# Adapter residual of the first pair: through memory as 32x32 squares instead of through TensorE

## Chip, cores and metric

One core of a Trainium2 chip runs the whole program. The metric is the device time of one execution in microseconds, the median of several runs. The engines work side by side, each through its own instructions in order: PE (TensorE, matrix products, with PEld for its weight loads), DVE (VectorE), ACT (ScalarE), POOL (GpSimd) and SP, which only issues transfers. Sixteen DMA engines move data between DRAM and the on-chip memory SBUF; matrix products land in the eight banks of PSUM.

## The reference

Four sequences of 512 tokens with 512 features pass through two layers. The first, in short:

```python
q, k, v = x @ Wq, x @ Wk, x @ Wv
attn_out = softmax(q @ k.T * scale) @ v @ Wp + bp
cms_out = gelu(attn_out @ cW1 + cb1) @ cW2 + cb2 + one_hot(target_codes)
modifier = gelu(concat([attn_out, cms_out]) @ mW1 + mb1) @ mW2 + mb2
out = clip(x + cms_out + modifier, 0, 1)
```

The second is an adapter with weights chosen per sequence (`stream`), and it is what the change touches:

```python
h = gelu(hidden_states @ Wd + bd)          # 512 -> 256
h = h @ Wu + bu                            # 256 -> 512
h = hidden_states + h                      # the residual
h = (h - mean) / sqrt(var + 1e-5) * g + b  # over the 512 features of a token
```

All data are float32.

## The kernel before

The four sequences are worked on in two pairs. After attention, each pair goes through four large layers (c1, c2, m1, m2 for cW1, cW2, mW1, mW2). Their products are made by a Strassen-like scheme: seven outer products p, in the order of `FIRST_C = (2, 1, 5, 6, 7, 3, 4)` for c1 and of `SECOND = (3, 1, 5, 6, 7, 2, 4)` for c2, each made of seven inner products q. A float32 product of 256 columns shows as two TensorE instructions in the profile. The activations are kept turned, features on the 128 partitions and tokens along the free dimension.

In the second pair's c1 layer each outer product is made by `c1_two_level` through `seven` (line 591). Per inner product TensorE writes two PSUM banks (rows r = 0, 1), in the order q = 1, 5, 6, 2, 7, 3, 4. Between them stands work of VectorE: `add(c15[r], ps, c1[r])` after q5, `add(y[r], x[r], c15[r])` after q6, which TensorE must await before q7 accumulates onto x, `add(v, x[r], c15[r])` after q7, which it must await before q4, and the adds of `keep` into the hidden blocks. In products 6 and 7 POOL adds as well (L1178), and it makes the weight sums of later products (L1140) and the token sums (L1087 to L1090). The first copies c1[r] are ACT's, except in products 3 and 4, where they are VectorE's (L612).

The adapters of the first pair run inside that layer. `adapters()` (L1718) gives a generator; `c1_layer` takes one step of it after q6, q7 and q4 of each product but the first, so steps 1 to 3 lie in product 1, 4 to 6 in product 5, 7 to 9 in product 6, 10 to 12 in product 7, 13 to 15 in product 3 and 16 to 18 in product 4. `adapter` (L1573) needs seven steps per sequence, and sequence 1 comes before sequence 0:

- two steps `down` (L1509): eight TensorE instructions of 512 columns each, then a gelu on ACT into g, which is `first`;
- one step `with_bias` (L1504): ACT adds b_up to the turned input, into the tile of the sequence in `cms`;
- four steps, one for each 128 tokens t: `up_product` (L1521) lets TensorE turn the 128x512 block of the residual into a PSUM bank by four products with the identity (L1526) and accumulates the up product onto it (L1531); `normalised` (L1558) reads the bank twice on VectorE, for the statistics (L1561, L1563) and for (h - mean) * g into `part` (L1564). `root` (L1544) takes one square root per tile on ACT, VectorE its reciprocal (L1566). For t < 3 `shifted` (L1552) scales on ACT (L1554), adds b on POOL (L1555), and POOL issues the output (L1556); for t = 3 VectorE does both (L1568) and POOL only issues (L1569).

ACT has to load a table whenever it changes between gelu and square root. The adapter weights of sequence 1 are in slot 4 and 5, those of sequence 0 in slot 6 and 7; the halves of slot 5 and 7 behind the first 1024 columns are free. The operand sums of the first c2 product are POOL's and go to slots 6 and 7 after product 3 (`second_operands`, L1331, by L206). The tile framework sets all semaphores and orders each engine's instructions by its own plan; `keep_in_program_order` pins an instruction in the order in which the code gives it. The transfers that the change adds go to POOL's and ACT's queues; those of the weights are SP's.

The second pair's own adapters, at the end of the program, use `adapter` and `last_adapter` and are not touched. `bias_rows` (L157) is a small tile for the biases of the first layer, turned once at the start by L168.

Of the kernel before, what the change touches and what calls it, by code (L numbers as in the profile page):

```python
# [1 line left out]

# [6 lines left out]
F32 = mybir.dt.float32  # L9
I32 = mybir.dt.int32  # L10
AF = mybir.ActivationFunctionType
ALU = mybir.AluOpType
# [6 lines left out]
def kernel(  # L19
# [38 lines left out]
    nc = tc.nc  # L58
# [3 lines left out]
    E, _, BN = W_down.shape  # L62
    P = 128
    NT = T // P
    NV = V // P
    NH = HID // P
    NB = BN // P
# [8 lines left out]
    const = ctx.enter_context(tc.tile_pool(name="const", bufs=1))  # L76
    small = ctx.enter_context(tc.tile_pool(name="small", bufs=4))
    spill = ctx.enter_context(tc.tile_pool(name="spill", bufs=1, space=DRAM))
    psum = ctx.enter_context(tc.tile_pool(name="psum", bufs=8, space=PSUM))

    def bank(name):
        return psum.tile([P, 512], F32, tag="bank", name=name)
# [7 lines left out]
    cms = [const.tile([P, 4, 512], F32, name=f"cms{i}") for i in range(2)]  # L90

    mod = [const.tile([P, 4, 512], F32, name=f"mod{i}") for i in range(2)]

    wide = const.tile([P, 8, 512], F32, name="wide")
    slot = [wide[:, 4 * i : 4 * i + 4, :].rearrange("p c n -> p (c n)") for i in range(2)]
    slot += [const.tile([P, 2048], F32, name=f"slot{i}") for i in range(2, 8)]
    wslot = [const.tile([P, 2048], F32, name=f"wslot{i}") for i in range(4)]
    part = const.tile([P, 4, 512], F32, name="part")
    first = const.tile([P, 2, 512], F32, name="first")
# [54 lines left out]
    bias_src = (bp, cb1, cb2, mb1, mb2)  # L154
    counts = [v.shape[0] // P for v in bias_src]
    nbias = sum(counts)
    bias_rows = const.tile([nbias, P], F32, name="bias_rows")  # L157
    at = 0
    for v, n in zip(bias_src, counts):
        nc.gpsimd.dma_start(  # L160
            out=bias_rows[at : at + n, :], in_=v.rearrange("(c p) -> c p", p=P)
        )
        at += n
    bias = const.tile([P, nbias], F32, name="bias")
# [18 lines left out]
    eps = const.tile([P, 1], F32, name="eps")  # L183
# [362 lines left out]
    def add(dst, a, b):  # L546
        nc.vector.tensor_tensor(dst, a, b, ALU.add)  # L547
# [220 lines left out]
        return left_operand(w, s)  # L768

    xT_kept = [spill.tile([P, 4, 512], F32, name=f"xT_kept{b}") for b in range(B)]  # L770
    attn_kept = [spill.tile([P, 4, 512], F32, name=f"attn_kept{b}") for b in range(B)]

    def softmax(k, lhs, rhs, then):
# [125 lines left out]
    ends = []  # L899
# [604 lines left out]
    def with_bias(y, bu, y1):  # L1504

        for c in range(NV):
            nc.scalar.activation(y1[:, c, :], y[:, c, :], AF.Identity, bias=bu[:, c : c + 1])

    def down(y, wd, bd, g, n, tokens=slice(0, 512)):  # L1509
        ps = bank("down_ps")[:, : tokens.stop - tokens.start]  # L1510
        for c in range(NV):
            nc.tensor.matmul(  # L1512
                ps,
                lhsT=wd[:, c, n * P : (n + 1) * P],
                rhs=y[:, c, tokens],
                start=(c == 0),
                stop=(c == NV - 1),
            )
        nc.scalar.activation(g[:, n, tokens], ps, AF.Gelu, bias=bd[:, n : n + 1])
# [53 lines left out]
    def adapter(b, y, loaded, g, rows, y1, eng):  # L1573
# [7 lines left out]
        for t in range(NT):  # L1581
            normalised(b, rows[:, t, :], up_product(g, wu, y1, t), aff, t, eng)
            yield

    def last_adapter(b, y, loaded, g, rows, y1, eng):


        wd, wu, bd, bu, aff = loaded
# [23 lines left out]
        for t in range(NT):  # L1612
            stats = small.tile([P, 2, 6], F32, name="stats")
            mv = small.tile([P, 2], F32, name="mv")
            pieces = []
            for i, columns in enumerate(both if t == NT - 1 else whole):
                ps = up_product(g, wu, y1, t, columns)
# [9 lines left out]
            rstd = scaled(t, pieces, mv)  # L1627
            if t == 0:
                shifted(b, rows[:, t, :], rstd, aff, t, eng)
            elif t == 1:  # L1630
                h = rows[:, t, :]
# [15 lines left out]
    def next_hidden():  # L1647

        h11, h12, h21, h22 = turned
        turned[:] = [h22, h11, h21, h12]  # L1650
        return list(turned)
# [5 lines left out]
    for pair in range(B // 2):  # L1657
        final = pair == B // 2 - 1

        h = next_hidden()  # L1660
# [21 lines left out]
        h = next_hidden()  # L1682
# [27 lines left out]
        loads = {}  # L1710
# [4 lines left out]
        def adapt(s, space, eng, pair=pair, loads=loads, kind=adapter):  # L1715
            return kind(2 * pair + s, cms[s], loads[s], *space, eng)

        def adapters(adapt=adapt):  # L1718
            for s in (1, 0):
                yield from adapt(s, (first, part, cms[s]), nc.gpsimd)  # L1720

        next_rhs = []

# [78 lines left out]
```

## Time and profile before

| | |
|---|---|
| median of three runs | 1170.36 us (1168.99 to 1171.34) |
| the profiled execution | 1169.93 us, of which its span 1168.2 us |
| instructions in it | 13,723 |
| mean granted TensorE clock | 0.999 |
| adapters of the first pair, from the first down to the last output issued | 693.8 to 784.9 us |
| end of the second pair's c1 layer on TensorE | 792.2 us |
| 128x128 turns by TensorE in this stretch (L1526) | 32 instructions |
| up products in it (L1531) | 32 instructions |
| ACT table loads at L1547 and L1039 in the whole program | 6 and 4, 1.28 us each |

Busy time is the time in which an engine has an instruction under way; TensorE's instructions overlap, so its busy time does not say that it runs at its peak, and the distance from the start of one group of instructions to the next is a better price. Idle time carries the name of what ended it. The timeline gives start and duration of instructions, neighbours of one line merged (x4 = four of them); the windows give the busy time of each engine in a stretch, with the number of instructions.

### The profile page before, as it was taken

Reading aid. Unit: us, or ns where it says so; the run is one execution under the profiler, and the core shown is the slowest. Engines: PE = TensorE matmul, PEld = TensorE weight load, DVE = VectorE, ACT = ScalarE, POOL = GpSimd, SP = SyncE. Lnnn points to the kernel's source line nnn. Section 1 sums busy time; section 2 is a strip of 40 time slices with the busy share of each in tenths; the row PEclk is TensorE's granted clock in tenths of the full one; section 3 lists DMA queues with packets and bytes.
Section 4 is the critical chain, followed back from the end, with each engine's and each line's share of the span. In section 5 each row is a group of like instructions: output and inputs, shape, how many; then the busy total and the mean of one; then the engine's idle time right before and its main releaser. Section 6 shows DMA issues by size and latency. Waiting matters only on the chain.

```text
span 1168.2 us, 13723 instructions
## 1 busy us (share of the span) xinstructions
PE 1158.7 (99%) x4989; PEld 927.4 (79%) x4989; DVE 893.8 (77%) x1215; ACT 293.2 (25%) x535; POOL 588.6 (50%) x652
## 2 busy tenths in 40 slices
PE   9999999999999999999999999999999999999997
PEld 8588558657468888888888887778888888888875
DVE  5755655587699967899699956689994588689956
ACT  4244315236520000012310027271000003220014
POOL 4989999988897058982200636972000001242101
PEclk9999999999999999999999999999999999999999
DMA  9742784897766588896847662135745454594701
GB/s 336 268 139 100 297 323 176 307 382 253 300 240 245 185 282 313 322 328 263 258 157 279 191 215 90 64 143 179 299 132 188 168 216 180 176 307 165 246 6 73
DMA packets 81283, 256.80 MB, mean 220 GB/s; under 512 B 7956, under 2 KB 38976, under 8 KB 65984
## 3 DMA queue, kind: packets, MB, share of 16 engines
q1 hardware_dynamic: 56864, 152.98, 36.4%
q0 software_dynamic: 21968, 93.37, 22.7%
q10 hardware_dynamic: 2384, 9.57, 2.1%
q8 instruction: 40, 0.66, 0.2%
q14 instruction: 27, 0.22, 0.1%
HBM read 186.69 MB, written 66.06 MB: 216 GB/s over the span
## 4 chain that ended last, share of the span: by engine, by line
PE 94%; DVE 2%; POOL 1%; DMA 1%; issue 1%; DVEq 0%
PE i L1406 29%; PE i L1306 26%; PE sum L1148 9%; PE sum L703 9%; PE sum L637 8%; PE c L1238 6%; PE down_ps L1512 2%; PE up_ps L1531 2%; PE tr_ps L489 1%; DMA wslot<-in_L_cond_mW 1%; PE up_ps L1526 1%; DVE slot L206 1%; DVE hidden L547 1%; PE tr_ps L868 0%; PE idle_ps L193 0%
## 5 line engine op out<-in xcount | busy, mean ns | idle before, releaser
L1306 PE MATMUL i<-slot,wslot 128*128 128x256 f32 x1184 | 261.4, 379 | 1.3 <-DVE part L1010 1.2
L1306 PEld LDWEIGHTS i<-slot,wslot 128*128 128x128 f32 x1184 | 224.7, 190 | 32.8 <-issue 1.8
L1406 PE MATMUL i<-slot,wslot 128*128 128x256 f32 x896 | 202.5, 379 | 0.0
L1406 PEld LDWEIGHTS i<-slot,wslot 128*128 128x128 f32 x896 | 170.2, 190 | 23.1
L1017 ACT COPY first<-i 128x256 f32<-128x256 f32 (+1 forms) x56 | 26.7, 477 | 516.0 <-PE i L1406 255.6
L1406 PE MATMUL i<-hidden,wslot 128*128 128x256 f32 x576 | 132.2, 379 | 0.0
L1406 PEld LDWEIGHTS i<-hidden,wslot 128*128 128x128 f32 x576 | 109.4, 190 | 15.7 <-issue 1.0
L1010 DVE TENSOR_TENSOR part<-i,part 128x512 f32<-128x512 f32 (+1 forms) x156 | 90.5, 591 | 37.7 <-PE i L1306 25.4
L1039 ACT ACTIVATE hidden<-hidden,bias 128x512 f32<-128x512 f32 x128 | 83.9, 716 | 81.3 <-DVE hidden L547 71.3
L1688 POOL DMA_DIRECT2D slot<-xT_kept x4 | 2.7, 683 | 152.9 <-PE i L1306 152.9
L1148 PE MATMUL sum<-mod,wslot 128*128 128x256 f32 x288 | 66.7, 379 | 0.2 <-DVE sum L547 0.2
L206 DVE TENSOR_TENSOR slot<-hidden 128x1024 f32<-128x1024 f32 x46 | 61.3, 1332 | 0.0
L1148 PEld LDWEIGHTS sum<-mod,wslot 128*128 128x128 f32 x288 | 54.6, 190 | 7.9 <-DVE sum L547 0.6
L1691 POOL TENSOR_TENSOR cms<-cms,slot 128x512 f32<-128x512 f32 x16 | 24.4, 1548 | 71.3 <-PE i L1306 41.1
L1010 DVE TENSOR_TENSOR part<-i,first 128x512 f32<-128x512 f32 (+1 forms) x62 | 36.3, 589 | 29.0 <-PE i L1306 17.7
L547 DVE TENSOR_TENSOR sum<-sum,wslot 128x512 f32<-128x512 f32 x48 | 33.3, 696 | 31.5 <-PE sum L703 19.6
L206 DVE TENSOR_TENSOR slot<-hidden,slot 128x1024 f32<-128x1024 f32 x46 | 56.8, 1234 | 0.3
L1238 PE MATMUL c<-slot,wslot 128*128 128x512 f32 x128 | 55.3, 592 | 0.0
L547 DVE TENSOR_TENSOR hidden<-part,hidden 128x2048 f32<-128x2048 f32 x20 | 54.6, 2732 | 0.5
L703 PE MATMUL sum<-hidden,wslot 128*128 128x256 f32 x232 | 53.4, 380 | 0.6 <-POOL wslot L201 0.6
L703 PEld LDWEIGHTS sum<-hidden,wslot 128*128 128x128 f32 x232 | 43.7, 190 | 6.7 <-POOL wslot L201 1.0
L1238 PEld LDWEIGHTS c<-slot,wslot 128*128 128x128 f32 x128 | 24.3, 190 | 30.6 <-issue 27.5
(338 smaller groups left out, 2129.3 us busy)
## 6 DMA issues: line engine op xcount, KB each, us to landing
wslot<-m_kept SPq DMA_DIRECT2D x48, 1024.0 KB
wslot<-m_kept SPq DMA_DIRECT2D x36, 512.0 KB
wslot<-c_kept SPq DMA_DIRECT2D x16, 1024.0 KB
slot<-in_L_cond_mW POOLq DMA_DIRECT2D x24, 512.0 KB
wslot<-in_L_cond_mW SPq DMA_DIRECT2D x24, 512.0 KB
wslot<-in_L_cond_cW SPq DMA_DIRECT2D x40, 256.0 KB
slot<-in_L_cond_cW POOLq DMA_DIRECT2D x16, 512.0 KB
m_kept<-wide POOLq DMA_DIRECT2D x6, 1024.0 KB
```

Source lines behind the costliest of these rows:

```text
L206: i = eng.tensor_tensor(out_, one, two, ALU.subtract)
L547: nc.vector.tensor_tensor(dst, a, b, ALU.add)
L637: nc.tensor.matmul(ps, lhsT=lhs[p][:, c, r * P : (r + 1) * P], rhs=rhs[p][:, c, :], start=(first_ and c == 0), stop=(c == 1), skip_group_c ...
L703: nc.tensor.matmul(v[:, j, :], lhsT=lhs[p][:, c, j * P : (j + 1) * P], rhs=rhs[p][:, c, :], start=(first_ and j == 0 and c == 0), stop=(c ...
L1010: nc.vector.tensor_tensor(dst, ps, other, ALU.add)
L1017: nc.scalar.copy(c1, p1)
L1039: nc.scalar.activation(block[:, t, :], block[:, t, :], AF.Gelu, bias=bias_c[:, 8 * half + t : 8 * half + t + 1],)
L1148: nc.tensor.matmul(halves_of(ps)[:, j, :], lhsT=a[g][:, at_[q], j * P : (j + 1) * P], rhs=rhs[q][:, 0, :], start=(first_ and j == 0), stop ...
L1238: nc.tensor.matmul(ps, lhsT=lhs(c, t), rhs=operands[p][:, c, :], start=(c == 0), stop=(c == 1),)
L1306: nc.tensor.matmul(out_ps[:, j, :], lhsT=a[j][q][:, c, :], rhs=now[q][:, c, :], start=(c == 0), stop=(c == 1),)
L1406: nc.tensor.matmul(ps[:, :256], lhsT=a[k // 2][q][:, k % 2, :], rhs=now[q][:, k, :], start=(k == 0), stop=(k == 3),)
L1691: nc.gpsimd.tensor_tensor(cms[s][:, d, :], cms[s][:, d, :], in_rows[3][:, d, :], ALU.add)
```

## The change

For the first pair the residual is no longer turned by TensorE. ACT adds b_up in place, POOL writes the turned sequence to a DRAM tile (`turn_kept`), and four loads issued from ACT, one for each 32 partitions, read it back such that each 32x32 square lies in the place that it has in the token-major block, but still mirrored. VectorE then turns the squares of a 128x512 block with one instruction and adds the up product from PSUM; statistics and scaling read SBUF afterwards. The sequences go in the order 0, 1, with both downs first. Mean and variance of the four tiles are gathered in one tile, and one square root and one reciprocal per sequence serve all four; the rest (`shifted`, for all four tiles now) follows while the next sequence's tiles are made, and in steps 15 to 17 for the last. g has a place of its own for each sequence, in the free halves of slots 5 and 7. The rows of sequence 1 go to the tile that held sequence 0. `bias_rows` becomes a part of `mod[1]`.

```diff
-    bias_rows = const.tile([nbias, P], F32, name="bias_rows")
+    bias_rows = mod[1][:nbias, 0, :P]
...
+    turn_kept = [
+        spill.tile([P, 4, 512], F32, name=f"turn_kept{k}").rearrange("p q n -> (p q) n")
+        for k in range(2)
+    ]
...
+    def load_squares(src, dst):
+        squares = src.rearrange("(i r) (d a c) -> a r d i c", r=32, a=4, c=32)
+        for a in range(4):
+            yield tc.keep_in_program_order(nc.scalar.dma_start(
+                out=dst[32 * a : 32 * a + 32].rearrange("p d (i c) -> p d i c", c=32),
+                in_=squares[a],
+            ))
+
+    def turned_adapters(two, space):
+        def first_half(b, y, loaded, g):
+            wd, wu, bd, bu, aff = loaded
+            for n in range(NB):
+                down(y, wd, bd, g, n)
+                if n == NB - 1:
+                    with_bias(y, bu, y)
+                    nc.gpsimd.dma_start(
+                        out=turn_kept[b % 2].rearrange("(c p) n -> p c n", p=P), in_=y
+                    )
+                yield
+
+        def reciprocal(rstd):
+            tc.keep_in_program_order(nc.vector.reciprocal(rstd, rstd))
+
+        def added(loaded, g, y, rows, t, mv):
+            wu, aff = loaded[1], loaded[4]
+            h = rows[:, t, :]
+            nc.vector.transpose(h, y[:, t, :])
+            ps = bank("up_ps")
+            for n in range(NB):
+                nc.tensor.matmul(
+                    ps, lhsT=g[:, n, t * P : (t + 1) * P], rhs=wu[:, n, :],
+                    start=(n == 0), stop=(n == NB - 1),
+                )
+            add(h, ps, h)
+            stats = small.tile([P, 6], F32, name="stats")
+            nc.vector.bn_stats(stats, h)
+            nc.vector.bn_aggr(mv[:, t, :], stats)
+            nc.vector.scalar_tensor_tensor(
+                h, h, mv[:, t, 0:1], aff[:, 0, :], ALU.subtract, ALU.mult
+            )
+
+        y1, y2 = two[0][1], two[1][1]
+        squares = chain(*(load_squares(turn_kept[b % 2], y) for b, y, _, _ in two))
+        yield from first_half(*two[0])
+        yield
+        for _ in first_half(*two[1]):
+            next(squares)
+            next(squares)
+            yield
+        yield
+        def end(n=1):
+            for _ in range(min(n, len(ends))):
+                ends.pop(0)()
+
+        ends = []
+        for i, rows in enumerate((space, y1)):
+            b, y, loaded, g = two[i]
+            mv = small.tile([P, NT, 2], F32, name="mvs")
+            for t in range(NT):
+                added(loaded, g, y, rows, t, mv)
+                if i == 0 and t < 2:
+                    next(squares)
+                    next(squares)
+                elif t == 2:
+                    end()
+                elif t == 3:
+                    end(4)
+                yield
+            rstd = small.tile([P, NT], F32, name="rstds")
+            nc.scalar.activation(rstd, mv[:, :, 1], AF.Sqrt, bias=eps)
+            ends = [partial(reciprocal, rstd)] + [
+                partial(shifted, b, rows[:, t, :], rstd[:, t : t + 1], loaded[4], t, nc.gpsimd)
+                for t in range(NT)
+            ]
+        yield
+        end()
+        yield
+        end(4)
...
-        def adapters(adapt=adapt):
-            for s in (1, 0):
-                yield from adapt(s, (first, part, cms[s]), nc.gpsimd)
+        def adapters(pair=pair, loads=loads):
+            g = [t[:, 1024:].rearrange("p (n k) -> p n k", n=NB) for t in (slot[5], slot[7])]
+            return turned_adapters(
+                [(2 * pair + s, cms[s], loads[s], g[s]) for s in (0, 1)], part
+            )
```

More of the change, by code (lines that the diff above doesn't have):

```diff
@@ L1 @@
 from contextlib import ExitStack
+from functools import partial
+from itertools import chain
 import concourse.bass as bass
```

## The prediction

> **What bounds the kernel now.** I read the page first, then the chain of waits, then the stretch in which the first pair's adapters run. Page, parts 1 and 4:
>
> ```profile
> PE 1158.7 (99%) x4989; PEld 927.4 (79%) x4989; DVE 893.8 (77%) x1215; ACT 293.2 (25%) x535; POOL 588.6 (50%) x652
> ...
> PE 94%; DVE 2%; POOL 1%; DMA 1%; issue 1%; DVEq 0%
> ```
>
> TensorE issues from end to end, so any TensorE instruction removed is worth its issue time, unless another engine takes the place. TensorE's timeline at one adapter tile gives that price (start, duration, line, operation; x4 = four instructions):
>
> ```profile
> 712.73 0.60 PE L1526 MATMUL up_ps<-ident,cms 128*128 128x128 f32 x4
> 713.17 1.88 PE L1531 MATMUL up_ps<-slot,first 128*128 128x512 f32 x4
> 714.89 1.89 PE L1148 MATMUL sum<-slot,wslot 128*128 128x256 f32 x8
> ```
>
> By starts, the four turns of a tile cost 713.17 - 712.73 = 0.44 us, the four up matmuls 714.89 - 713.17 = 1.72 us, and eight of the first layer's instructions 1.73 us. The windows of the last four products of the second pair's first layer (p = 6, 7, 3, 4) and of the layer behind show who stands next to TensorE (columns: PE, PEld, DVE, ACT, POOL busy, clock, DMA share, GB/s):
>
> ```profile
> 726.11:747.22 21.11, 21.11 (x82) 14.83 (x81) 15.34 (x25) 6.36 (x10) 20.29 (x23) 1.00 0.30 111
> 747.22:763.61 16.39, 16.39 (x73) 12.94 (x72) 9.94 (x16) 6.47 (x10) 16.16 (x19) 1.00 0.16 48
> 763.61:780.13 16.52, 16.52 (x73) 12.86 (x72) 14.51 (x29) 12.11 (x18) 14.22 (x18) 1.00 0.17 62
> 780.13:792.22 12.09, 12.09 (x57) 10.64 (x56) 11.97 (x22) 7.66 (x12) 7.86 (x5) 1.00 0.90 295
> 792.22:804.31 12.09, 12.09 (x58) 10.64 (x57) 12.09 (x11) 4.66 (x8) 2.98 (x2) 1.00 0.55 167
> ```
>
> VectorE has idle time in the first three (5.8, 6.4, 2.0 us) and none in p = 4 or behind it; POOL is 96 to 99% busy in the first two; the DMA engines are nearly empty until p = 4.
>
> **The change, part by part.** The sum is made against the profiled execution: span 1168.2 us, 1169.93 us as a run, 0.4 us under the median of 1170.36; differences are added to the median.
>
> *Turns removed.* 8 tiles x 0.44 = 3.5 us off TensorE. Nothing else of TensorE changes: 4 down products and 8 x 1.72 us of up matmuls stay, in another order: products 1 and 5 now hold all four downs (3.43 us each), products 6, 7, 3 hold 3, 3 and 2 tiles. Products 6 to 4 then take 4 x 12.08 + 8 x 1.72 = 62.1 us instead of 66.1.
>
> *VectorE per tile.* Today a tile costs these rows:
>
> ```profile
> 715.63 0.68 DVE L1561 BATCH_NORM_STATS2 stats<-up_ps 128x6 f32<-128x512 f32 x1
> 716.35 0.18 DVE L1563 BATCH_NORM_AGGREGATE mv<-stats 128x2 f32<-128x6 f32 x1
> 716.57 0.75 DVE L1564 SCALAR_TENSOR_TENSOR part<-up_ps,mv,slot 128x512 f32<-128x512 f32 x1
> ```
>
> That is 0.72 + 0.22 + 0.67 (start to start where back to back), plus a reciprocal of 0.15, and one shift of 0.74 to 1.64 per sequence (L1568). New are a transpose and an add from PSUM. The add is L547's: pairs take 1.28, so 0.61. No VectorE transpose is in this trace: the lower bound is 0.34 (half of the 0.68 of the 128x1024 TENSOR_SCALAR at L1467), the upper two passes, 1.22; I take 0.61, the one-source COPY of the same shape (L612, 0.66 to 0.68, 0.60 start to start). A new tile is 0.61 + 0.61 + 1.59 = 2.8 us.
>
> The Trainium skill ("VectorE: DVE Perf Modes", The three transpose paths, and its rules for authors) lists 311 ns for a 128x128 bf16 VectorE transpose and advises TensorE for 128x128 where PSUM may be the target, which speaks against this change. Four of its figures would be an estimated 1.24 us, and the sum below would be 5 us higher; no run so far shows which holds.
>
> *The scaling operation changes its source.* L1564 reads one SBUF tensor and PSUM today; now it reads two SBUF tensors. Two rows of the same operation with two SBUF tensors differ by what POOL does beside them:
>
> ```profile
> 736.43 1.64 DVE L1568 SCALAR_TENSOR_TENSOR part<-part,rstd,slot 128x512 f32<-128x512 f32 x1
> 783.32 0.74 DVE L1568 SCALAR_TENSOR_TENSOR part<-part,rstd,slot 128x512 f32<-128x512 f32 x1
> ```
>
> At 736.43 POOL was adding (L1178), at 783.32 it was idle. So each of the scalings can cost 0 to 0.9 us more; I take half, 0.45, for the six tiles of products 6 and 7, where POOL hardly rests: 2.7 us.
>
> *VectorE's account.* The first layer's own work in products 6 to 4 is 64 adds x 0.605 + 4 copies x 0.62 = 41.2 us. With 8 x 2.81 and two reciprocals it becomes 64.0, with contention 66.7. It can begin 2.6 us into product 6 (the first c15 add follows three half products of 0.86) and may end 2.1 us after TensorE, as today (792.22 against 794.36): 62.1 - 2.6 + 2.1 = 61.6 us. So it is 5.1 us over (2.4 without contention). Today the tiles of one sequence fell into product 5, which has idle time; the new order puts downs there and all eight tiles behind it. A further 1.5 us: VectorE waits for the up matmuls of a tile it is due to add, as it does now (three waits for up_ps, 3.4 us, between 726 and 795; about half taken).
>
> *Slack behind.* The second layer starts with a long block of pinned VectorE work, and its eight PSUM banks come back late (VectorE, then TensorE):
>
> ```profile
> 802.16 4.48 DVE L1326 TENSOR_TENSOR hidden<-hidden,hidden 128x2048 f32<-128x2048 f32 x2
> 806.56 0.41 DVE L1010 TENSOR_TENSOR cms<-i,cms 128x256 f32<-128x256 f32 x1
> 806.90 0.41 DVE L1010 TENSOR_TENSOR cms<-i,first 128x256 f32<-128x256 f32 x1
> ...
> 806.03 5.34 PE L1406 MATMUL i<-slot,wslot 128*128 128x256 f32 x24
> ```
>
> TensorE needs another bank at 806.03 + 2 x 1.73 = 809.5; the first one that this burst returns is free at 807.3. VectorE can be 2.2 us later than today before TensorE stops.
>
> *The detour through memory.* POOL issues two 1 MB writes, 0.56 us each as at L1556. ACT issues eight loads, 0.51 us each (the four of Wk took 2.06). Each load has 32 x 4 x 16 = 2048 runs of 128 bytes, 128 per DMA engine. The rows around that size: 80 packets of 4 bytes took 1.2% of 16 engines in 350 to 355 us, 12 ns each; 558 of 1 KB took 51.5% in 3 to 6 us, 44 ns each. So one load is 1.5 to 5.7 us of all engines; nearest is the small end, 16 ns, 2.1 us. The first sequence's last two loads stand behind its partner's bias on ACT: product 5 starts at 707.55, the second down ends at 707.55 + 8.63 + 2 x 3.43 = 723.0, gelu 0.69 and four times 0.72 end at 726.6, issue 1.0, then 2.2 us until data is usable (the first Wq quarter: issued 0.73, read 4.45, less 1.5 us for its and Wk's 0.5 MB at the 350 GB/s of that window), then 4.2 us: 734.0. The first tile is due when product 6 has run three of its seven parts, 726.5 + 5.2 = 731.7. Late by 2.3 us, which I take; bounds 1.2 (3.1 us of data) to 9.4 (11.3). What waits behind the first transpose on VectorE are product 6's remaining adds, and TensorE waits for these before q7. ACT, waiting for the second write, holds nothing until product 7's copies.
>
> The Trainium skill ("DMA: Bandwidth & Descriptors", Specifications) puts full line rate at 512 bytes and more, with read-modify-write below; the 4-byte row shows no such penalty in its record. By the page I would take the far end, 9.4 us late, and the sum would be 7.1 us higher.
>
> *At nothing:* six square roots and some four table loads less (1.28 us each, ACT is 39 to 73% busy in these products; no gain on the path either, though VectorE's two waits for rstd, 3.6 us, end); two more POOL adds and the moved output DMAs (POOL waits 5.3 us before L1569 today; without that cover the operand sums, 784.9 to 795.2, run later and could cost 2 us); the first down now needs cms0, complete at 681.5, for 693.8; bias_rows in mod1 (its transpose is done at 23.2, mod is first written at 26.1).
>
> **Sum.** -3.5 + (5.1 + 1.5 + 2.3 - 2.2) = +3.2 us: 1170.4 + 3.2 = **1173.6 us**.
>
> **The rivals.** *TensorE keeps its gain* (24%): the transposes move into VectorE's idle time, contention stays out, loads are in time. Then 2.4 us over is covered by the 2.2 us and the time is 1170.4 - 3.5 = 1166.9. For it: no wait of TensorE in this stretch today, and the deferred roots take VectorE's 3.6 us of waits away; against it: the account without any mishap already uses the slack up. *The gain is given back at the second layer* (12%): VectorE reaches 794.4 as today and paces what follows; 1170.4. For it: the 100% busy window behind 792. *The squares are slow* (14%): 1 KB-like packets or a write that waits behind POOL's sums (710.6 to 720) make the first tile 9.4 us late instead of 2.3: 1173.6 + 7.1 = 1180.7. It decides from a load time of 4 us each. Against it: empty DMA engines. That the turns don't vanish from TensorE has no ground: up_product isn't called on this path.
>
> **How the numbers follow.** The forecast, VectorE as bound of products 6 to 4, has 50%, from 1170.5 to 1178 (more contention, 8 x 0.9, gives +4.5; a transpose of 1.22 gives +3.7 on six tiles). About 0.2%, 2.3 us, is what a measurement tells from no change. Of the 50%, 13 lie below 1172.7; with the 12% that is 25% for the same; faster 24%; slower 37 + 14 = 51%. The range takes in the full gain with 1.1 us below it (the runs before lie 1.4 us under their median) and the slow loads up to their price: 1165.8 to 1180.8.
>
> **What would show it.** Right: L1526's first-pair instructions gone; VectorE above 95% busy from about 732 to 790; TensorE waiting for L547 or for a PSUM bank there; scalings with a spread from 0.74 to 1.6. Squares: ACT's loads land after VectorE's first transpose is due, and that wait is named DMA. Wrong: VectorE idle for more than 3 us in products 6 and 7, or TensorE without gaps up to 850 us and the whole 3.5 us won.

## The result and the profile after

The changed kernel takes 1173.48 us (median of 16 runs, 1171.06 to 1176.03), the kernel before 1168.95 us in its own 16 (1167.68 to 1171.34). The ratio is 1.0037, 95% interval 1.0028 to 1.0045: about 4.3 us slower. The profiled execution has a span of 1172.7 us against 1168.2. Lines move by a few: L547 is L549 now, L1148 is L1154, L1406 is L1412, L206 is L208, L1326 is L1332; the new lines are L1620 (transpose), L1623 (up product), L1629 and L1630 (statistics), L1631 (scaling), L1560 and L1561 (root's factor on ACT, b on POOL).

The turns are gone: TensorE runs 4957 instructions where it ran 4989, and product 6 begins at 726.56 us, 0.45 us later than before, as the two downs more and three tiles less ahead of it require (2 x 3.43 - 3 x 2.16 = 0.4). Then the windows of the stretch: product 6, product 7 up to the end of the wait and somewhat beyond, and the rest of 7 with half of 3 (columns: PE, PEld, DVE, ACT, POOL busy, clock, DMA share, GB/s):

```profile
726.00:743.20 17.20, 17.20 (x69) 12.92 (x68) 12.07 (x21) 4.03 (x8) 14.49 (x17) 1.00 0.71 153
743.20:760.50 17.30, 12.78 (x46) 9.61 (x45) 17.09 (x28) 5.07 (x7) 14.69 (x17) 0.86 0.32 90
760.50:776.00 15.50, 15.50 (x56) 11.20 (x56) 13.63 (x25) 4.46 (x7) 13.61 (x15) 0.93 0.16 51
```

Of these three, VectorE is full in the second alone. TensorE loses 4.5 us there, and its granted clock is under 1.00 in that window and the next, which it was nowhere in this stretch before. TensorE's timeline shows one wait (in brackets: idle before, and what ended it):

```profile
750.69 1.89 PE L1154 MATMUL sum<-slot,wslot 128*128 128x256 f32 x8
757.10 3.78 PE L1154 MATMUL sum<-mod,wslot 128*128 128x256 f32 x8 [4.52 <-DVE sum L549]
760.67 2.42 PE L1154 MATMUL sum<-slot,wslot 128*128 128x256 f32 x6
```

The same eight instructions take 1.89 us before the wait and 3.78 after it. VectorE's timeline shows what it did while TensorE waited:

```profile
747.03 1.29 DVE L1620 STREAM_TRANSPOSE part<-cms 128x512 f32<-128x512 f32 x2
...
749.87 1.81 DVE L1631 SCALAR_TENSOR_TENSOR part<-part,mvs,slot 128x512 f32<-128x512 f32 x1
...
753.26 0.78 DVE L1631 SCALAR_TENSOR_TENSOR part<-part,mvs,slot 128x512 f32<-128x512 f32 x1
753.97 1.29 DVE L1620 STREAM_TRANSPOSE cms<-cms 128x512 f32<-128x512 f32 x2
755.19 1.24 DVE L549 TENSOR_TENSOR mod<-sum,mod 128x512 f32<-128x512 f32 x2
756.36 1.28 DVE L549 TENSOR_TENSOR sum<-sum,mod 128x512 f32<-128x512 f32 x2
```

The last two rows are product 7's c15 and y additions, the ones TensorE needs for q7. In the code they stand ahead of the fourth tile and of the second sequence's transposes; the framework's plan has put both in front. So the 4.5 us are a matter of order as well as of load. The windows behind the wait, TensorE alone (busy, instructions, clock, DMA share, GB/s):

```profile
756.00:758.00 2.00, 0.90 (x2) 0.50 0.00 0
...
762.00:764.00 2.00, 2.00 (x7) 0.85 0.00 0
```

The fourteen instructions behind the wait take 762.93 - 757.10 = 5.8 us where 14 x 0.216 = 3.0 were due: 2.8 us that no part of the prediction had. From the first down to the start of c2 (the second pair's second layer) TensorE needs 102.30 us, before it was 98.44. The account: -3.5 for the turns, 4.5 to 4.7 for the wait (idle time, and from start to start), 2.8 for the clock, sum +3.8 to +4.0, measured +3.86. The rest, +0.65, lies in c2 and behind. There the new order leaves the second sequence's four b additions to POOL at the start of c2, beside VectorE's first operands:

```profile
798.27 3.92 DVE L1332 TENSOR_TENSOR wide<-hidden,hidden 128x2048 f32<-128x2048 f32 x1
802.11 2.28 DVE L208 TENSOR_TENSOR slot<-hidden 128x1024 f32<-128x1024 f32 x1
...
807.88 1.23 DVE L208 TENSOR_TENSOR slot<-hidden 128x1024 f32<-128x1024 f32 x1 [1.28 <-POOL cms L1561]
```

Before, the first took 3.00 and L206 1.21 each time, with no wait. VectorE's block behind them starts 14.0 us into c2 instead of 9.9.

The squares were in time. The first sequence's last load landed at 731.81 us, VectorE's first transpose ran at 732.55 with no wait for a DMA, and the DMA view of 700 to 760 us has:

```profile
q10 hardware_dynamic: 16512, 2.10, 22.3%
...
cms<-turn_kept ACTq DMA_DIRECT2D x8, 256.0 KB, 4.3
```

0.223 x 60 us x 16 engines / 16512 packets is 13 ns for a packet of 128 bytes, and the median load lands 4.3 us after its issue. The slowest took 9.5 us (740.09 to 749.57) and was still 4.4 us ahead of its transposes.

### The profile page after: what moved, and what is told of

Read it like the earlier page. It is cut to its first block, busy times and chain, and to the rows that moved or that the text cites. A ratio compares the mean times of both kernels' runs of the same rounds, so it can differ in the third digit from the quotient of the medians.

```text
span 1172.7 us, 13683 instructions
## 1 busy us (share of the span) xinstructions
PE 1158.0 (99%) x4957; PEld 925.6 (79%) x4957; DVE 898.7 (77%) x1223; ACT 288.3 (25%) x527; POOL 598.4 (51%) x656
## 4 chain that ended last, share of the span: by engine, by line
PE 84%; POOL 8%; DMA 3%; DVE 3%; issue 2%; SPq 0%; DVEq 0%; POOLq 0%
PE i L1312 28%; PE i L1412 27%; PE sum L639 7%; PE sum L1154 6%; PE c L1244 6%; PE sum L705 5%; PE down_ps L1518 2%; DMA wslot<-in_L_cond_mW 1%; PE up_ps L1537 1%; DMA c_outer<-part 1%; PE tr_ps L491 1%; POOL slot L208 1%; DMA wide<-in_L_cond_Wq 1%; POOL wide L200 1%; POOL wslot L1146 0%
## 5 line engine op out<-in xcount | busy, mean ns | idle before, releaser
L1412 PE MATMUL i<-slot,wslot 128*128 128x256 f32 x896 | 202.5, 379 | 0.0
L1412 PEld LDWEIGHTS i<-slot,wslot 128*128 128x128 f32 x896 | 170.2, 190 | 23.1
L1412 PE MATMUL i<-hidden,wslot 128*128 128x256 f32 x576 | 132.3, 379 | 0.1
L1412 PEld LDWEIGHTS i<-hidden,wslot 128*128 128x128 f32 x576 | 109.4, 190 | 16.2 <-issue 1.0
L1154 PE MATMUL sum<-mod,wslot 128*128 128x256 f32 x288 | 68.5, 387 | 4.5 <-DVE sum L549 4.5
L1154 PEld LDWEIGHTS sum<-mod,wslot 128*128 128x128 f32 x288 | 55.7, 194 | 13.1 <-DVE sum L549 4.9
L208 DVE TENSOR_TENSOR slot<-hidden 128x1024 f32<-128x1024 f32 x46 | 63.5, 1380 | 1.3 <-POOL cms L1561 1.3
L549 DVE TENSOR_TENSOR sum<-sum,wslot 128x512 f32<-128x512 f32 x48 | 33.3, 696 | 33.1 <-PE sum L705 21.2
L208 DVE TENSOR_TENSOR slot<-hidden,slot 128x1024 f32<-128x1024 f32 x46 | 57.4, 1248 | 0.2
L549 DVE TENSOR_TENSOR hidden<-part,hidden 128x2048 f32<-128x2048 f32 x20 | 48.0, 2399 | 0.5
```

Source lines behind the costliest of these rows:

```text
L208: i = eng.tensor_tensor(out_, one, two, ALU.subtract)
L1154: nc.tensor.matmul(halves_of(ps)[:, j, :], lhsT=a[g][:, at_[q], j * P : (j + 1) * P], rhs=rhs[q][:, 0, :], start=(first_ and j == 0), stop ...
L1412: nc.tensor.matmul(ps[:, :256], lhsT=a[k // 2][q][:, k % 2, :], rhs=now[q][:, k, :], start=(k == 0), stop=(k == 3),)
```

## Experiments

Three theories. **Order:** the plan makes the wait, the wait makes the low clock; mend the order and some 7 us come back. **Load:** VectorE has too much to do from product 6 on, and a mended order only moves the wait. A third took shape later: what VectorE does too slowly is the **scaling**, which now reads two tiles in SBUF while POOL works. The table gives all runs. Each ratio is to executions of the kernel before that were taken beside that kernel (their medians lie between 1168.88 and 1169.90 us), so the kernels are better compared by it than by their medians. Two columns split each profiled execution on TensorE: first down to start of c2, and start of c2 to its last instruction. What lies ahead differs by up to 4 us between executions of the same code (the first down begins between 691.2 and 695.5 us), which the two columns leave out.

| kernel | median us | ratio to before (95%) | to c2 | c2 to end |
|---|---|---|---|---|
| before | 1168.95 | | 98.44 | 369.62 |
| changed | 1173.48 | 1.0037 (1.0028 to 1.0045) | 102.30 | 370.27 |
| transposes pinned | 1171.63 | 1.0022 (1.0012 to 1.0031) | 99.35 | 370.98 |
| squares from SyncE | 1177.15 | 1.0064 (1.0051 to 1.0077) | 105.50 | 371.04 |
| no detour | 1168.62 | 0.9991 (0.9981 to 1.0001) | 96.03 | 371.02 |
| TensorE turns again | 1170.89 | 1.0013 (1.0004 to 1.0021) | 98.32 | 370.58 |
| kernel before, with fills | 1177.23 | 1.0065 (1.0050 to 1.0080) | 106.22 | 369.62 |
| root per tile, second sequence | 1172.74 | 1.0026 (1.0015 to 1.0036) | 100.78 | 373.04 |
| early squares | 1172.77 | 1.0029 (1.0019 to 1.0039) | 100.73 | 370.96 |
| c1 copies on ACT | 1172.81 | 1.0026 (1.0017 to 1.0036) | 98.53 | 372.80 |
| additions pinned | 1172.78 | 1.0034 (1.0022 to 1.0046) | 101.50 | 371.07 |
| no b, second sequence | 1170.34 | 1.0008 (0.9998 to 1.0018) | 99.75 | 370.04 |
| one sequence turned | 1180.84 | 1.0099 (1.0083 to 1.0114) | 108.84 | 369.62 |
| sum left in PSUM | 1168.46 | 0.9994 (0.9985 to 1.0003) | 95.80 | 370.99 |

**Transposes pinned** (in `added`):

```diff
-            nc.vector.transpose(h, y[:, t, :])
+            tc.keep_in_program_order(nc.vector.transpose(h, y[:, t, :]))
```

> The eight transposes keep their place in program order, so the additions of y that TensorE waits for in product 7 are no longer behind the third tile's chain and a later tile's transposes; nothing else is edited. Theory 1 (the order makes the stall, and the stall makes the low clock): TensorE's wait on L549 in product 7 falls from 4.5 us to under 1 us, the clock after it stays near 1.00, both costs (4.5 and 2.8 us) go, and the kernel takes some 7 us less than the changed one: 1166 to 1168 us, below the kernel before. Theory 2 (VectorE simply has too much work in products 7 to 4): VectorE is as full as before, the wait moves to a later product, and the time stays within 1 us of the changed kernel's 1173.5.

Both theories were partly right, and the time met neither's range. The 4.5 us wait is gone and the clock stays at 1.00 throughout, 2.95 us less to the start of c2. But VectorE has no gap from 746 us to the end of c1, and TensorE waits three times in products 3 and 4:

```profile
771.58 1.99 PE L1154 MATMUL sum<-mod,wslot 128*128 128x256 f32 x8 [1.98 <-DVE sum L549]
785.04 1.99 PE L1154 MATMUL sum<-slot,wslot 128*128 128x256 f32 x8 [1.12 <-DVE mod L614]
787.44 1.99 PE L1154 MATMUL sum<-mod,wslot 128*128 128x256 f32 x8 [0.41 <-DVE sum L549]
```

3.5 us of waits stand where 4.5 us and the clock stood: the saving of the turns is still all spent. The following kernels start from this one unless told otherwise.

**Squares from SyncE**, on the changed kernel (`nc.sync.dma_start` in `load_squares` instead of `nc.scalar`):

> The loads of the mirrored squares are issued by SyncE and no longer by ScalarE. On ScalarE the issues took 0.57 to 1.93 us each and stood before the scaled copies of the products. Theory 1, as far as the order is planned from ScalarE's load: the planned order puts the y additions of product 7 ahead of the third tile's work, the 4.5 us wait and the low clock go: 1166 to 1168 us. Rival: SyncE carries the weights too, and a load of squares that waits for its write holds them up; TensorE then waits for weights instead, 1172 to 1178 us. Theory 2 (total work of VectorE): no change, 1173.5 within 1 us.

The rival held. Product 7's additions did come ahead of the fourth tile in the plan, but TensorE waits for POOL's weight sums, the waits view says:

```profile
PE sum L1154 <- POOL wslot L1146: 7.1, 3, 3.7
```

SP carries the weights; a load of squares stands in its queue until the write has landed, and the weights behind it are late.

**No detour**, on the changed kernel (no write, no loads):

```diff
-                    nc.gpsimd.dma_start(
-                        out=turn_kept[b % 2].rearrange("(c p) n -> p c n", p=P), in_=y
-                    )
...
-        squares = chain(*(load_squares(turn_kept[b % 2], y) for b, y, _, _ in two))
+        squares = iter(range(8))
```

> Leaves out the write of the first layer's input to memory and the loads of the mirrored squares: the residual that is added is the tile as it stands, not its mirror. All instructions of VectorE and TensorE stay. Theory 1: without ScalarE's issues the plan has the y additions first, and the stall goes: 1165 to 1168 us. Theory 2 (VectorE's work is the bound whatever the order): within 1 us of 1173.5, since none of VectorE's work is gone. If the detour's transfers themselves were what costs, it would be near 1169 with the stall in product 7 still there.

Near the expectation of the order theory (1168.6 for 1165 to 1168), but not by order alone: with nothing to wait for, all eight transposes ran between 704.6 and 727.4 us, where VectorE is otherwise idle, 8 x 0.6 = 4.8 us out of the full stretch. TensorE waits 0.7 us in c1 and reaches c2 2.4 us sooner than in the kernel before. By this run, what the detour costs is the late place of the transposes. The scalings were no faster here: 9.5 us for the eight, against 8.0 in the changed kernel.

**TensorE turns again** (on the changed kernel: `up_product` in `added`, no write, loads or transposes):

> The residual is turned by TensorE again as in the kernel before (four 128x128 turns in each tile's product), with no write, no loads, no transposes and no third addition of the tile; what stays of the change is the order of the sequences and the one square root per sequence. The turned part alone is undone. Theory 1 and 2 both: no stall at product 7, TensorE has its 3.5 us of turns back. If the order and the single root are worth nothing, 1169 to 1170.5; if the fewer table loads of ScalarE matter, 1167 to 1169; if the later order of the two sequences alone makes a wait, over 1171.

1170.89, between the bounds given for "worth nothing" and for a wait. Up to c2 it is level with the kernel before, with no wait. The excess, +0.96 us, lies in c2, where VectorE again waits 1.3 us for L1561 and TensorE 0.7 for VectorE. So the new order with its single root costs about 1 us, with or without turned squares.

**Kernel before, with fills** (nothing of the change):

```diff
+        if p == 7 and beside is not None:
+            for _ in range(9):
+                tc.keep_in_program_order(nc.vector.memset(slot[7][:, 1024:], 0.0))
```

> The kernel before, with nine fills of an unused 128x1024 area on VectorE, pinned ahead of product 7's additions; none of the change is in it. They hold up the y additions for which TensorE waits, by an estimated 4 us. In the changed kernel TensorE's one wait of 4.5 us was followed by a granted clock of 0.50 and some 2.8 us more. If the wait itself makes the clock fall, whatever causes it: a wait of about 4 us in product 7, then a clock near 0.50 for some 4 to 6 us, and the kernel some 6 to 7 us over the kernel before. If the low clock came from something else in the change (the transfers, the transposes), the clock stays 1.00 after the wait and the kernel is only the wait longer, 3 to 4 us.

The fills held TensorE up in product 7 by 0.24 us only, since the plan put just four of them ahead of the additions and spread the rest between the adds. But the plan behind them changed too, and at an adapter tile of product 3 TensorE waited 4.6 us for VectorE, which itself stood 4.3 us behind ACT's root. For the question that does as well, and the clock falls with none of the change in the kernel (TensorE's timeline, then its windows):

```profile
779.98 1.09 PE L1529 MATMUL up_ps<-ident,cms 128*128 128x128 f32 x4 [4.60 <-DVE rstd L1569]
780.86 3.62 PE L1534 MATMUL up_ps<-slot,first 128*128 128x512 f32 x4
```
```profile
780.00:782.00 2.00, 2.00 (x6) 0.50 0.34 131
```

The four up matmuls take 3.62 us for 1.88, and the kernel is 7.6 us over. The wait makes the low clock, as the order theory said.

**Root per tile, second sequence** (abridged):

```diff
+                elif i == 1:
+                    end((0, 7, 2, 2)[t])
+                    rstd = root(mv[:, t, :])
+                    ends += [
+                        partial(reciprocal, rstd),
+                        partial(shifted, b, rows[:, t, :], rstd, loaded[4], t, nc.gpsimd),
+                    ]
```

> The changed kernel with pinned transposes, and the second sequence with one square root per tile again, so that its tiles are scaled, added to and stored while the next are made, and not all four at the start of c2. Theory (the single root is what costs about 1 us in c2): POOL's four b additions no longer lie beside VectorE's first operands of c2, VectorE's wait of 1.3 us on L1561 and TensorE's wait of 0.8 us on L1016 go, and the kernel is 0.7 to 1.3 us faster than with pinned transposes alone: 1170.3 to 1171 us. Rival: VectorE has no idle time in products 3 and 4, and its three more reciprocals and the additions of POOL beside its scalings cost there what c2 gives back: 1171.6 or more.

The rival held, on both sides of c2: waits of 1.5 and 2.6 us in products 3 and 4, and in c2 0.8 us for POOL's operand sums (L208) and 1.5 us for VectorE. POOL has the same work whichever end it is put at.

**Early squares:** the first sequence's four loads together ahead of the second's first down, its four transposes in one place ahead of product 6 (abridged).

```diff
-        for _ in first_half(*two[1]):
-            next(squares)
-            next(squares)
-            yield
+        second = first_half(*two[1])
+        for n in range(NB):
+            if n == 0:
+                for _ in range(4):
+                    next(squares)
+            next(second)
+            yield
+        for t in range(NT):
+            turned(y1, space, t)
```

> Pinned transposes, with the first sequence's four loads issued one step earlier together, and its four transposes in one place ahead of product 6's additions (some 724 to 729 us), where VectorE was idle for 5 us; nothing is left out or added. Theory 2 as it now stands (once the order is mended, VectorE has no idle time from 734 us to the end of c1, and each us of work moved out of that stretch is worth up to a us): 2.0 us of transposes leave the stretch, and the kernel is 1.2 to 2 us faster than with pinned transposes alone: 1169.6 to 1170.4 us. Rival (only the order counts): 1171.6 within 0.5. If the squares arrive later than 729 us, the transposes hold up product 6's additions instead and TensorE waits there: 1172 to 1174.

The four transposes ran at 728.72 in 2.48 us, in VectorE's idle time as intended. Nothing was gained, because the plan again put two tiles ahead of product 7's additions, and TensorE waited 2.7 us there; 2.1 us more of waits lie in products 3 and 4. Order decided; the theory of load was not tested by it.

**c1 copies on ACT** (products 3 and 4):

```diff
-        copy = nc.vector.tensor_copy if p in (3, 4) else nc.scalar.copy
+        copy = nc.scalar.copy
```

> Pinned transposes, with the c1 copies of products 3 and 4 made by ScalarE (as they are in the other products) and not by VectorE: 4 instructions of 0.65 us less on VectorE, right where TensorE's waits of 2.0 and 1.1 us lie. Theory 2: 2.6 us less work in VectorE's full stretch, and these waits shrink; 1.5 to 2.5 us faster than with pinned transposes alone: 1169.1 to 1170.1 us. Rival: ScalarE is held by its gelu and its table loads there, the copies come later than VectorE's would, and nothing is gained: 1171.6 or more.

Half each. Product 3's wait of 2.0 us is gone. In product 4 the plan took the two banks apart and put other adds ahead of the first y, for which TensorE waits 2.1 us; the second bank's copy comes at 787.09, behind two table loads and four gelus on ACT, and costs 0.6 us. Another 0.5 us of wait is in product 7, and in c2 TensorE waits 1.4 us for VectorE.

**Additions pinned** (early squares, with `add(h, ps, h)` in program order too, and only product 3's copies on ACT):

> The early squares again, but with each tile's addition of the up product pinned too, and the c1 copies of product 3 (not of product 4) made by ScalarE. With early squares alone a chain of two tiles was planned ahead of product 7's additions (TensorE waited 2.7 us); with all copies on ScalarE the 2.0 us wait of product 3 went and one of 2.1 us came in product 4, where ScalarE's copy came after two table loads and eight gelus. Theory (what is left is order plus VectorE's load, and both yield): the 2.7 and 2.0 us waits go, about 1.5 us of waits are left in products 7 to 4, and the kernel takes 1169 to 1170.3 us. Rival (VectorE's total decides): the waits turn up again elsewhere, 3 us or more in all, 1171.5 or more.

The wait in product 7 is gone, and ahead of c2 only two waits are left, in product 3:

```profile
769.25 1.13 PE L1154 MATMUL sum<-wide,wslot 128*128 128x256 f32 x4 [2.34 <-ACT mod L614]
771.17 3.78 PE L1154 MATMUL sum<-mod,wslot 128*128 128x256 f32 x8 [0.79 <-DVE sum L549]
```

The first is ACT's copy, which came at 768.63 behind gelus that had waited for POOL. The clock was halved once more (1.89 became 3.78), from 770.4 us on: after the first of the two and as the second began. The total came out as the rival said, by a mechanism that neither had named.

**No b, second sequence** (transposes pinned; POOL's additions of b to the second sequence left out):

```diff
+        if b != 1:
+            nc.gpsimd.tensor_tensor(h, h, aff[:, 1, :], ALU.add)
```

> Pinned transposes; leaves out POOL's four additions of b to the second sequence (its output lacks b). In all variants so far with one root per sequence these additions lie at the start of c2, behind POOL's operand sums, while VectorE makes its first operands there, and c2 and what follows take 1.0 to 1.4 us longer than in the kernel before. Theory (these additions are that cost): VectorE's wait on L1561 and TensorE's 0.8 us wait in c2 go, c2 and what follows are within 0.4 us of the kernel before, total 1170.2 to 1170.9 us. Rival (something else in c2): 1171.6 within 0.5.

The theory held. VectorE's operands in c2 are back to 3.15 and 1.21 us, its wait and TensorE's are gone, c2 and what follows take 370.04 us: 0.94 less than with pinned transposes, 0.42 over the kernel before.

**One sequence turned** (the changed kernel's tiles for sequence 1, the old ones for sequence 0 behind it; transposes and additions pinned, one root per tile; abridged):

```diff
+        for t in range(NT):
+            pinned_(nc.vector.transpose(tiles[:, t, :], y1[:, t, :]))
+        with_bias(y0, loaded0[3], y0)
+        yield
+        for t in range(NT):
+            turned_tile(t)
+            yield
+        for t in range(NT):
+            normalised(
+                b0, y1[:, t, :], up_product(g0, loaded0[1], y0, t), loaded0[4], t, nc.gpsimd
+            )
```

> Half the change: sequence 1 first, its residual through memory and turned by VectorE; sequence 0 after it as in the kernel before, turned by TensorE; one root per tile for both, as before. TensorE saves 16 turns, 4 x 0.44 = 1.75 us, VectorE's extra work is half as much, four transposes lie in its idle time before product 6, and nothing is left for the start of c2. Theory (VectorE's stretch and the late end took what TensorE saved): no wait of TensorE over 0.5 us in products 6 to 4, nothing added in c2, and the kernel is 1.2 to 1.8 us under the kernel before, 1167.4 to 1168.2 us where that takes 1169.4. Rival (any such work on VectorE gives the saving back): 1169 to 1170.5.

The expectation failed by 13 us, and this run showed what two SBUF sources can cost. TensorE waited 2.67 and 4.85 us for additions behind two of the scalings, and each time its clock was halved for 3.4 us. VectorE's timeline, then POOL's:

```profile
743.30 5.45 DVE L1570 SCALAR_TENSOR_TENSOR part<-part,mv,slot 128x512 f32<-128x512 f32 x1
...
752.50 7.42 DVE L1570 SCALAR_TENSOR_TENSOR part<-part,mv,slot 128x512 f32<-128x512 f32 x1
```
```profile
752.67 1.28 POOL L1184 TENSOR_TENSOR hidden<-hidden,hidden 128x512 f32<-128x512 f32 x1
753.90 1.42 POOL L1146 TENSOR_TENSOR wslot<-wslot 128x256 f32<-128x256 f32 x2
755.26 0.73 POOL L1093 TENSOR_TENSOR mod<-slot 128x256 f32<-128x256 f32 x1
755.94 2.75 POOL L1146 TENSOR_TENSOR wslot<-wslot 128x256 f32<-128x256 f32 x4
758.66 0.71 POOL L1094 TENSOR_TENSOR mod<-slot,mod 128x256 f32<-128x256 f32 x1
```

The scaling, 0.74 us alone, takes 7.42 us. It ends at 759.92, just after POOL's unbroken run ends at 759.37; the other ends at 748.75, POOL's run before it at 748.19. But POOL need not rest for a scaling to get through. In the changed kernel the one that ran from 749.87 to 751.68 ended 0.55 us after one addition of POOL, which went straight on until 756.67:

```profile
749.86 1.27 POOL L1184 TENSOR_TENSOR hidden<-hidden,hidden 128x512 f32<-128x512 f32 x1
751.08 1.19 POOL L1146 TENSOR_TENSOR wslot<-wslot 128x256 f32<-128x256 f32 x1
```

So did the changed kernel's five others beside POOL's additions, each 0.55 us after the end of the addition under way at its start. The two long ones ended 0.55 us after the sixth and the ninth. Why those were passed over so often is not shown. The scaling with a source in PSUM never waited: in the kernel before the eight took 0.74 to 0.75 us, five of them with POOL busy from their start to their end.

**Sum left in PSUM** (early squares and pinned additions, copies as before; statistics and scaling read the bank):

```diff
-            add(h, ps, h)
+            tc.keep_in_program_order(nc.vector.tensor_tensor(ps, ps, h, ALU.add))
...
-            nc.vector.bn_stats(stats, h)
+            nc.vector.bn_stats(stats, ps)
...
-                h, h, mv[:, t, 0:1], aff[:, 0, :], ALU.subtract, ALU.mult
+                h, ps, mv[:, t, 0:1], aff[:, 0, :], ALU.subtract, ALU.mult
```

> Early squares and pinned additions of the tiles, all c1 copies of products 3 and 4 on VectorE as in the kernel before, and the sum of residual and up product is left in the PSUM bank, so that statistics and scaling read it there (one SBUF operand beside it, as in the kernel before) and not two tiles in SBUF. With two SBUF operands the scaling took 0.74 to 1.81 us in the changed kernel, and 5.45 and 7.42 us in the half change, ending as POOL's run of work ended; with PSUM it took 0.745 us in the kernel before, beside a POOL as busy. Theory (the scaling's second SBUF operand is held up by POOL): all eight scalings take 0.73 to 0.80 us, VectorE has some 2.5 us less to do from 734 us on than with pinned transposes, TensorE's waits in products 7 to 4 fall from 3.5 to under 1.5 us, and the kernel takes 1168.5 to 1170 us; what is left over the kernel before is c2's 1.0 to 1.4 us. Rival (the banks, now held to the end of the scaling, come free too late for the next up products): TensorE waits for banks at the up products, 1171.5 or more.

As expected, with the time just under its range. The scaling's line (count, then shortest, median and longest in ns), and the waits of TensorE from 690 to 900 us:

```profile
L1635 DVE SCALAR_TENSOR_TENSOR part<-up_ps,mvs,slot x4: 737/739/750, 738.0 to 755.0; 128x512 f32<-128x512 f32 x4
L1635 DVE SCALAR_TENSOR_TENSOR cms<-up_ps,mvs,slot x4: 736/738/740, 762.3 to 780.1; 128x512 f32<-128x512 f32 x4
```
```profile
PE i L1412 <- DVE cms L1016: 0.8, 1, 0.8
PE sum L1154 <- DVE sum L549: 0.4, 1, 0.4
```

TensorE reaches c2 after 95.80 us, 2.6 us sooner than before; c2 and what follows take 1.37 us more. The kernel is 5 us below the changed one and level with the kernel before (interval -0.15% to +0.03%). It differs from the kernel with additions pinned in two things, the PSUM source and product 3's copies; the eight equal scalings show the first, the absent wait for ACT the second, but not what each is worth in time.

## Why the prediction was right, and where it was not

The forecast was 1173.6 and slower, with VectorE as the bound of products 6 to 4; measured 1173.48. The side is right and the bound is VectorE, but the agreement of the sum is partly luck: the forecast was +3.2 us on a median of three, 1170.36; the measured difference is 4.3 (by the ratio) to 4.5 us on a median of 16, 1168.95. In the terms, too, errors cancel.

- *Turns, -3.5:* right. No detour and sum left in PSUM, where hardly a wait is left, reach c2 2.4 and 2.6 us sooner than before, with 0.7 and 0.4 us of waits beside it.
- *Transpose, 0.61:* right: 0.60 start to start where four stand together, 0.70 alone. The 1.24 us per tile that was estimated from the Trainium skill's figure ("VectorE: DVE Perf Modes", The three transpose paths) is not what this trace shows.
- *VectorE over by 5.1 us, waiting 1.5 for its up matmuls:* the sign is right, the form is not. VectorE waited 1.2 us for them, but TensorE did not lose the overhang bit by bit: in the plan chosen it lost one wait of 4.5 us in product 7. With the order mended it lost 3.5 us in products 3 and 4. The prediction took VectorE's order from the code, though the text ahead of it had said that the framework plans it; that is the step that failed. (The rows of a tile today add up to 1.61 us, not 1.59: 0.2 us over eight tiles.)
- *Scaling with two SBUF sources, 0 to 0.9 us more each, 2.7 taken:* the mechanism is right, and the eight cost 8.0 - 8 x 0.74 = 2.1 us more. The upper bound is wrong by far: 6.7 us more in one sequence turned. It was read off one row and taken for a surcharge; it is a wait for the end of an addition of POOL, mostly of the one under way, twice (in one sequence turned) of a much later one. What it is worth in time no run isolates: early squares with pinned additions and the copies on VectorE was not run, and might do without the PSUM source. No detour is as fast as sum left in PSUM (0.9991 and 0.9994) with slow scalings. Common to the two is that VectorE has less to do in the full stretch than in the changed kernel: 4.8 us of transposes less and 1.5 us of scalings more in the one, 2.4 us of transposes and 2.1 us of scalings less in the other.
- *Squares 2.3 us late:* wrong, no wait at all. The time of the issue was right (726.6 said, 726.8 and 727.4 measured) and so was the packet (16 ns, measured 13). What was mis-sized is the way from issue to landing: 1.0 + 2.2 + 4.2 = 7.4 us for the two loads, measured 731.81 - 726.77 = 5.0. (Of the 80 packets read as 4 bytes, half were of 32.) By the Trainium skill's rule of 512 bytes ("DMA: Bandwidth & Descriptors", Specifications) the prediction would have put them 9.4 us late; the trace shows nothing of the kind.
- *Slack of 2.2 us in c2:* it was nearer 3.7 (with pinned transposes VectorE's block came 4.8 us later into c2 than before, and c2 took 1.1 us longer on TensorE; in the changed kernel 4.1 and 0.35), and it was used up by something costed at nothing: the four b additions of POOL. The prediction named 2 us should their cover go; leaving them out gave 0.94 us back.
- *Not in the prediction:* the clock, 2.8 us. With it the account is -3.5 + 4.6 + 2.8 + 0.65, where the prediction had -3.5 + 5.1 + 1.5 + 2.3 - 2.2.
- *Rivals:* that TensorE keeps its gain is close to what sum left in PSUM does up to c2, and that the second layer takes it back to what the same kernel does behind it (2.6 us gained, 1.4 lost). Squares that are slow are excluded by the landing times.
- *Signs:* the turns are gone, TensorE waited for VectorE's additions (L549), and the scalings spread from 0.74 to 1.81 us. VectorE was 93% busy from 732 to 790 us, not above 95. A sign named for "wrong" was also there: VectorE was idle for 4.6 us in product 6, 2.9 of them ahead of its first addition at 729.41, and for 2.0 us in product 7, behind the wait.

Open: whether c2 can be freed as well. Without the b additions it was, but no kernel here both computes them and has them out of the way; the one attempt, a root per tile, made POOL's operand sums late. Not tried either is the last kernel with its sum in SBUF and nothing else changed, which would price the PSUM source by itself.

## What to carry to other kernels

Before work is moved onto an engine, look at which two operands each of its instructions will then read: beside a busy POOL the same scaling took 0.73 to 7.42 us here with two SBUF sources, and 0.74 to 0.75 with one of them in PSUM. Where a framework plans the order, an account of busy time is not enough; pin the instructions that the bottleneck waits for, and look in the trace at what stands in front of them. A single wait of TensorE of 3.7 us or more cost more than its length here, one of 2.3 to 2.7 us sometimes; three short ones, 3.5 us in all, left the clock alone.

## What the runs showed of the hardware

*The clock after a wait.* Waits of TensorE in which, or up to 1.1 us behind which, the granted clock fell to 0.50: 4.5 us (changed), 4.6 (fills), 3.7 (squares from SyncE), 2.34 (additions pinned), 2.67 and 4.85 (one sequence turned). Waits that left it at 1.00: 2.72 (early squares), 2.65 (root per tile), 2.0 (transposes pinned). So from 2.3 to 2.7 us it can go either way, and length alone does not decide. The low clock lasted 6.8 us each time, in one sequence turned twice 3.4. In the 3.41 us ahead of each fall TensorE had been busy for 0.2 to 1.1 us. The Trainium skill ("TensorE: Matmul & The Clock Gate", Part 1) has the clock halve after an idle window of some 3.4 us that runs freely. The lengths of 3.4 and 6.8 us fit one and two such windows, and a free window fits the two outcomes at one length; but a fall after an idle time of 2.34 us, with TensorE busy for the rest, is earlier than its figure.

*VectorE beside POOL.* With two SBUF sources the same 128x512 operation took 0.73 to 7.42 us, and ended 0.55 us after the end of an addition of POOL wherever it was held up; transposes and statistics, which read one SBUF source or PSUM, kept to 0.71 and 0.70 us in the same stretch. The Trainium skill ("SBUF — State Buffer", SBUF: two separate sides) tells of a port pair that VectorE and GpSimd lock for a whole instruction, and names two SBUF inputs as one of the cases. The changed kernel's rows agree: none waited longer than one addition of POOL takes, 1.3 us at most there. Two rows of one sequence turned do not: there VectorE was passed over until the sixth and the ninth addition in a row had ended.

*A plan is not local.* Nine fills in product 7 changed the order of work in the product behind it, and moving four loads and four transposes put two tiles in front of product 7's additions, where pinned transposes alone had left no wait.
